# A third attention head of a graph layer turned by 32x32 squares and transfers, in half-head pieces

## The chip, the cores and the metric

The kernel runs on one core of a Trainium2 chip. TensorE (PE) multiplies matrices and transposes, VectorE (DVE) and ScalarE (ACT) work element by element and empty TensorE's accumulation banks (PSUM), GpSimd (POOL) does some additions, and SyncE (SP) issues the transfers (DMA). Times are device microseconds of one launch. The median of three runs before is 3433.64 us, and the runs lie between 3432.25 and 3434.13.

## The reference, cut to what matters

A batch of 32 graphs, each with 512 nodes and 256 channels, passes four layers of graph attention. After each layer the input is added and the sum is normalised over its channels:

```python
x = _layernorm(x + _L0_gnn_ref(x, adj, ...))   # "a": one head of 256 channels
x = _layernorm(x + _L1_gnn_ref(x, adj, ...))   # "b": transformer, 8 heads of 32
x = _layernorm(x + _L2_gnn_ref(x, adj, ...))   # "c": 4 heads of 64
x = _layernorm(x + _L3_gnn_ref(x, adj, ...))   # "d": bilinear scores, one head
```

The change is mainly in the third layer, c:

```python
q = (h @ W).reshape(B, N, H, D)                # H = 4, D = 64
e = e_src[:, :, None, :] + e_dst[:, None, :, :]
e = jnp.where(e >= 0, e, ALPHA * e)
e = jnp.where(mask, e, NEG_INF)
attn = jax.nn.softmax(e, axis=2)
h_prime = jnp.einsum('bijh,bjhd->bihd', attn, q)
```

For each head there is a 512 x 512 matrix of attention weights. The kernel holds it as four row blocks of 128 x 512. The last line sums over its columns, and TensorE sums over the partitions, so each of the four blocks has to be transposed before the weighted sum: this is what the kernel calls turning.

## The kernel before, in words

All values are float32. The program builds a list of operations (`op`), each with the engines that may run it, a planned cost, the buffers that it writes and reads, and a stage name: a letter for the layer and a digit (0 preparation, 1 scores, 2 finish, 3 softmax and turning, 4 weighted sum). `Plan.order` then lays the operations out engine by engine, with up to `WINDOW` = 4 graphs in work at once. Among ready operations it takes the one with the lowest key: graph number times `AGE` of the engine, less the length of the chain behind it, less `URGENT` of engine and stage; for TensorE a change of the matmul's form (full, tiled by rows, tiled by columns) costs `SWITCH_WEIGHT` times an entry of `SWITCH`. An operation that takes a buffer waits in the plan until one of the `BUFS` of its kind is free. The result is a fixed order for every engine; on the chip the engines follow their own lists and wait for each other by semaphores.

In layer c, `Gat.attend` (line 814) goes over two groups of two heads. For each head TensorE spreads a column of scores over a bank (line 835), VectorE adds the mask and takes each row's maximum (`masked`, line 684), and ScalarE applies the leaky slope (line 739) and the exponential (line 745) in place. Then `turned` (line 691) transposes in one of two ways:

- By TensorE: `turn` (line 580) makes four 128 x 128 transposes into a bank for each row block (line 586), and `copied` takes the bank to the turned buffer `pq` (ScalarE at line 529 or VectorE at line 531, as the planner decides).
- By squares and transfers: VectorE transposes every 32 x 32 square in place (line 702), once for each row block, and SyncE moves the squares to their places with 16 transfers of 64 KB for a head (line 714). Each transfer waits for all four row blocks, since a head's four blocks are one buffer `tq`, which is held from the masking until the last transfer has landed.

`BY_TRANSFERS` names the heads that go the second way: heads 2 and 3 of layer c, in all graphs but the last `PLAIN` = 2. A turned head is one `pq` buffer of 2048 words per partition. `weighted` (line 591) then multiplies for both heads of a group, four row blocks at once: 512 columns, in two column tiles of 64 side by side (line 603). The sum is copied to `oT`, transposed back for each half of the nodes (`turned_back`, line 610, instructions at line 619), and scaled into `y` (line 631). Layers a and d use `rows_weighted` (line 890, instructions at line 896), layer b `weighted` with 256 columns in four tiles of 32. Other lines that the numbers below name: 557 and 572 are projections, 806 the projection of layers a and c, 934 the scores of layer b and 948 and 955 their masking and exponential, 1072 the scores of layer d. SyncE also loads the inputs (line 358) and stores the output (line 1108), in the same order as the moves.

Of the kernel before, what the change touches and what calls it, by code (L numbers as in the profile page):

```python
# [24 lines left out]
SLOPE = 0.2  # L25


BUFS = dict(t=16, x=5, xT=3, v=5, qk=4, y=5, e=3, n=2, nT=2, hT=3, oT=2, tq=2, pq=5, small=8)
# [11 lines left out]
AGE = {"PE": 257, "ACT": 221, "DVE": -182, "POOL": 528, "SP": 151}  # L40
URGENT = {
    "PE": {"a0": -75, "a1": 707, "a2": 344, "b0": -756, "b1": 306, "b2": 700, "c0": -1085, "c1": -566, "c2": -26, "d0": -1544, "d1": -1472, "d2": -1512, "a3": 1865, "a4": 679, "b3": 269, "b4": -122, "c3": 3149, "c4": 468, "d3": -1054, "d4": 94},
    "ACT": {"a0": -877, "a1": 23, "a2": 412, "b0": 1122, "b1": 150, "b2": 22, "c0": 432, "c1": -809, "c2": -763, "d0": 680, "d1": -1928, "d2": -1182, "a3": 920, "a4": 701, "b3": 234, "b4": -604, "c3": 1629, "c4": 1505, "d3": -786, "d4": -337},
    "DVE": {"a0": 633, "a1": 670, "a2": 648, "b0": 1045, "b1": -236, "b2": -513, "c0": -2048, "c1": -657, "c2": 497, "d0": -1572, "d1": -869, "d2": -2025, "a3": 1551, "a4": 544, "b3": -1617, "b4": -331, "c3": 91, "c4": 1954, "d3": -1641, "d4": -1168},
    "POOL": {"a0": -1566, "a1": -815, "a2": 2482, "b0": 1576, "b1": -742, "b2": -986, "c0": -744, "c1": -1896, "c2": 3131, "d0": 1272, "d1": 1709, "d2": -1760, "a3": -1181, "a4": 746, "b3": -824, "b4": 1874, "c3": -105, "c4": 2168, "d3": 1794, "d4": 2316},
    "SP": {"a0": 578, "a1": -291, "a2": 1436, "b0": -478, "b1": -110, "b2": -662, "c0": -380, "c1": -1000, "c2": 35, "d0": 1115, "d1": -375, "d2": -249, "a3": 144, "a4": 71, "b3": -603, "b4": 627, "c3": -231, "c4": 1331, "d3": 989, "d4": -515},
# [6 lines left out]
SWITCH_WEIGHT = 869  # L53
# [5 lines left out]
DMA_US = 0.63  # L59
# [3 lines left out]
BY_TRANSFERS = {"a": (), "b": (), "c": (2, 3), "d": ()}  # L63
# [247 lines left out]
def gnn_stack(  # L311
# [188 lines left out]
    class Rows:  # L500


        def __init__(self, buf, cell=None):
            self.buf, self.cell = buf, cell
            self.use = buf if cell is None else (buf, cell)

        def __call__(self):
            return self.buf[:] if self.cell is None else self.buf[:, self.cell]

    def rows(n, name, together=False):  # L510

        if together:
            t = buf("tq", [P, n, N], name, n)
            return [Rows(t, i) for i in range(n)]
        return [Rows(buf("t", [P, N], f"{name}_{i}")) for i in range(n)]
# [64 lines left out]
    def turn(t, pT, pcell, to, name):  # L580

        ps = bank([P, NB, P], name)

        def issue(e):
            for j in range(NB):
                nc.tensor.transpose(ps[:, j], t()[:, block(j)], ident)  # L586

        op({PE: 0.44}, issue, [ps], [t.use], [pT])
        copied(N, to, lambda: ps[:], [(pT, pcell)], [ps])
# [20 lines left out]
    def turned_back(oT, n, y, name, f=None):  # L610


        ps = bank([P, FB, n, P], f"{name}_o")

        def issue(e):
            for i in range(FB):
                for c in range(n):
                    o = oT[:, c, block(i)] if f is None else oT[:, f * FB + i]
                    nc.tensor.transpose(ps[:, i, c], o, ident)  # L619

        op({PE: 0.225 * n}, issue, [ps], [oT], [y])
        return ps
# [57 lines left out]
    def masked(s, t, top, i):  # L680


        def issue(e):
            nc.vector.tensor_tensor_reduce(  # L684
                out=t(), in0=s[:], in1=neg[:, i], scale=1.0, scalar=LOWEST, op0=ALU.add,
                op1=ALU.max, accum_out=top[:, i : i + 1],
            )

        op({DVE: 0.61}, issue, [t.use, (top, i)], [s, (neg, i)])

    def turned(ts, pT, blocks, by_transfers, name):


        if not by_transfers:
            for i in blocks:
                turn(
                    ts[i], pT, i, lambda i=i: pT[:, i * NB : (i + 1) * NB], f"{name}_tr{i}"
                )
            return

        for i in blocks:
            op({DVE: FLIP_US}, lambda e, t=ts[i]: nc.vector.transpose(t(), t()), [ts[i].use], [])
        t = ts[0].buf

        def squares():
            return t[:].rearrange("p i (j n) -> p (i j) n", n=P)

        for a in range(P // SQ):
# [6 lines left out]

            op({SP: P // SQ * DMA_US}, move, [(pT, a)], [t], lag=2.0)

    def leaky_softmax(ts, top, v, src, total, at, blocks, name):
# [17 lines left out]
        for i in blocks:  # L736

            def leaky(e, i=i, t=ts[i]):
                nc.scalar.activation(  # L739
                    t(), t(), AF.Prelu, alpha=SLOPE,  # L740
# [3 lines left out]
            def exp(e, i=i, t=ts[i]):  # L744
                nc.scalar.activation(  # L745
                    t(), t(), AF.Exp, bias=bias[:, i : i + 1],
# [3 lines left out]
            op({ACT: 0.53 if src is None else 0.62}, leaky, [ts[i].use], [] if src is None else [v])  # L750
            op({ACT: 0.71}, exp, [ts[i].use, (total, at * NB + i)], [bias])
# [30 lines left out]
    class Gat(Layer):  # L782
# [31 lines left out]
        def attend(self):  # L814
            H, D, name, v = self.H, C // self.H, self.name, self.v
            G = min(H, P // D) if H > 1 else 1
            for g in range(0, H, G):
# [3 lines left out]
                for h in range(G):  # L821
# [5 lines left out]
                    ts = rows(NB, f"{name}_t{g}{h}", by_transfers)  # L827
                    pT = buf("pq", [P, NB * NB, P], f"{name}_pT{g}{h}", NB)
# [8 lines left out]
                    o = op({PE: 0.44}, issue, [dst], [v], [t.buf for t in ts])  # L837
# [6 lines left out]
                    turned(ts, pT, range(NB), by_transfers, f"{name}_{g}{h}")  # L844
                    pTs.append(pT)
                op({DVE: 0.1}, lambda e, a=inv, b=total: nc.vector.reciprocal(a[:], b[:]), [inv], [total])
                plan.stage = name[0] + "4"
                if H > 1:
                    pv = bank([P, N], f"{name}_pv{g}")
                    oT = buf("oT", [P, NB, P], f"{name}_oT{g}")  # L850
                    weighted(
                        pv, oT, pTs,
                        lambda h, j, pTs=pTs: pTs[h][:].rearrange(
                            "p (i j) n -> p i j n", j=NB
                        )[:, :, j],
                        v, g * D, D, 3.55,
                    )
                    copied(
                        N, lambda oT=oT: oT[:].rearrange("p i n -> p (i n)"), lambda pv=pv: pv[:],
                        [oT], [pv],  # L860
                    )
                for f in range(F):
                    y = self.part_y(f)
                    plan.stage = name[0] + "4"
                    if H > 1:
                        ps = turned_back(oT, 1, y, f"{name}_{g}{f}", f)
                        op({DVE: 0.4}, scaled(y, f, g * D, ps, inv, D), [y], [ps, inv])
                    else:
                        pv = bank([P, FB, C], f"{name}_pv{f}")
                        rows_weighted(pv, pTs[0], v, y, f)  # L870
# [19 lines left out]
    def rows_weighted(pv, pT, v, y, f):  # L890

        for i in range(FB):

            def issue(e, i=i):
                for j in range(NB):
                    nc.tensor.matmul(  # L896
                        pv[:, i], lhsT=pT[:, (f * FB + i) * NB + j], rhs=v[:, j, 0:C],
# [3 lines left out]
            reads = pT if BY_TRANSFERS[y.name[0]] else (pT, f * FB + i)  # L901
            op({PE: 1.73}, issue, [pv], [reads, v], [y])

    class Transformer(Layer):
# [14 lines left out]
        def attend(self):  # L919
            name, q_sb, k_sb = self.name, self.q, self.k  # L920
            for f in range(F):
# [4 lines left out]
                for c in range(NC):  # L926
                    ts = [rows(Q, f"{name}_t{f}{c}{i}") for i in range(FB)]
                    for i in range(FB):
                        ss = [bank([P, N], f"{name}_s{f}{c}{i}{q}") for q in range(Q)]

                        def scores(e, i=i, ss=ss, c=c, f=f):
# [8 lines left out]
                            {PE: 0.95}, scores, ss, [(q_sb, f), k_sb], [t.buf for t in ts[i]],  # L940
                            form="rows",
                        )
                        for q in range(Q):
# [3 lines left out]
                            def reduce(e, i=i, h=h, t=t, s=s, f=f, low=low):  # L947
                                nc.vector.tensor_tensor_reduce(  # L948
                                    out=t(), in0=s[:], in1=neg[:, f * FB + i],
# [4 lines left out]
                            def exp(e, i=i, h=h, t=t, low=low, total=total):  # L954
                                nc.scalar.activation(  # L955
                                    t(), t(), AF.Exp, bias=low[:, i, h : h + 1], scale=-1.0,
# [241 lines left out]
```

## Time and profile before

| | us |
|---|---|
| median of three runs | 3433.64 |
| time of the profiled execution | 3431.66 |
| its span, from first to last instruction | 3429.9 |
| TensorE busy | 3397.8 |
| VectorE busy | 2922.9 |
| ScalarE busy | 2785.3 |
| GpSimd busy | 854.4 |
| share of the 16 DMA engines' time taken by transfers that SyncE issued | 16.0% |

"Busy" is the time in which an engine had at least one instruction under way. For TensorE that is no measure of use: its matmuls overlap, and a matmul's mean time in a row is longer than the distance between two of them. "PEld" is its weight load, which runs beside the matmuls. A row of an instruction group gives line, engine, operation, what is written from what, shapes and count, then busy time and the mean of one instruction, then the idle time of the engine just before such instructions and what ended it. In a view by order of time a line has the start, the time from the first start to the last end, the engine, and the instructions merged into it. SyncE's lines give the time that the issue of a transfer took there; the transfer itself lands later.

### The profile page before, as it was taken

How to read it: one execution, taken by the hardware profiler on the slowest of the kernel's cores; microseconds unless marked ns; L12 is line 12 of the kernel's file. 1: busy time of each engine (PE TensorE's matmuls, PEld its weight loads, DVE VectorE, ACT ScalarE, POOL GpSimd, SP SyncE). 2: the span in 40 equal slices, each digit the busy share in tenths (PEclk: the TensorE clock that was granted, in tenths of full speed). 3: DMA queues.
4: the chain of work that ended last, by engine and by line, in shares of the span. 5: the costliest groups of instructions: out<-in, count | busy, mean ns of one | idle time of the engine just before them, and what ended most of it. 6: DMA issues, size and time to landing. Idle time of an engine off the chain costs nothing.

```text
span 3429.9 us, 65651 instructions
## 1 busy us (share of the span) xinstructions
PE 3397.8 (99%) x22744; PEld 2531.6 (74%) x22744; DVE 2922.9 (85%) x8645; ACT 2785.3 (81%) x6747; POOL 854.4 (25%) x840
## 2 busy tenths in 40 slices
PE   8999999999999999999999999999999999999998
PEld 6766777777777777777777777777777777777766
DVE  7889888888888888898888888888888889888886
ACT  6788788888788888888787888878888888878785
POOL 1222132222222222222223222222222222222322
PEclk9999999999999999999999999999999999999999
DMA  2012111121121220112211112102122011221100
GB/s 95 11 26 44 30 28 36 40 44 37 20 43 33 44 44 18 39 32 44 44 31 26 37 39 44 38 19 44 32 44 44 18 39 32 44 44 31 26 20 19
DMA packets 563787, 122.17 MB, mean 36 GB/s; under 512 B 510848, under 2 KB 562688, under 8 KB 563456
## 3 DMA queue, kind: packets, MB, share of 16 engines
q1 hardware_dynamic: 563456, 117.98, 16.0%
q8 instruction: 181, 2.97, 0.4%
q14 instruction: 150, 1.23, 0.1%
HBM read 38.21 MB, written 16.78 MB: 16 GB/s over the span
## 4 chain that ended last, share of the span: by engine, by line
PE 97%; ACT 1%; DVE 1%; DMA 1%; issue 0%; SPq 0%; POOL 0%; POOLq 0%; DVEq 0%; ACTq 0%
PE ps L586 21%; PE ps L603 14%; PE ps L896 13%; PE ps L557 13%; PE ps L572 10%; PE ps L934 8%; PE ps L806 7%; PE ps L1072 6%; PE ps L542 3%; PE ps L835 2%; PE ps L619 2%; ACT tq L745 0%; ACT t L739 0%; ACT pq L529 0%; DMA xT<-in_x_T 0%
## 5 line engine op out<-in xcount | busy, mean ns | idle before, releaser
L586 PEld LDWEIGHTS ps<-ident,t 128*128 128x128 f32 x6208 | 696.7, 141 | 221.7 <-ACT t L955 72.8
L955 ACT ACTIVATE t<-t,low 128x512 f32<-128x512 f32 x1024 | 737.5, 732 | 132.6 <-DVE low L948 132.6
L586 PE MATMUL ps<-ident,t 128*128 128x128 f32 x6208 | 824.2, 276 | 6.1 <-ACT t L745 5.5
L529 ACT COPY pq<-ps 128x512 f32<-128x512 f32 x1054 | 573.1, 588 | 240.6 <-PE ps L586 239.9
L676 POOL TENSOR_TENSOR y<-y,x 128x512 f32<-128x512 f32 x256 | 328.1, 1282 | 1563.3 <-DVE y L631 676.8
L948 DVE CUSTOM_DVE_ANT_0 t<-ps,neg 128x512 f32<-128x512 f32 x1024 | 646.2, 683 | 50.5 <-PE ps L934 50.2
L656 POOL TENSOR_TENSOR rstd<-rstd,mhalf 128x2 f32<-128x2 f32 x384 | 281.3, 733 | 843.3 <-DVE rstd L653 827.5
L603 PE MATMUL ps<-pq,v 128*32 128x256 f32 (+1 forms) x5120 | 490.2, 425 | 0.6 <-issue 0.4
L896 PE MATMUL ps<-v,pq 128*128 128x256 f32 x2048 | 473.4, 379 | 0.7 <-ACT pq L529 0.7
L896 PEld LDWEIGHTS ps<-v,pq 128*128 128x128 f32 x2048 | 377.1, 190 | 47.7 <-ACT pq L529 1.1
L603 PEld LDWEIGHTS ps<-pq,v 128*32 128x32 f32 (+1 forms) x5120 | 210.5, 115 | 254.9 <-issue 127.2
L531 DVE COPY pq<-ps 128x512 f32<-128x512 f32 x498 | 326.4, 678 | 56.2 <-PE ps L586 55.9
L745 ACT ACTIVATE t<-t,bias 128x512 f32<-128x512 f32 x528 | 373.5, 708 | 0.1
L684 DVE CUSTOM_DVE_ANT_0 t<-ps,neg 128x512 f32<-128x512 f32 x528 | 338.2, 681 | 15.5 <-PE ps L1072 11.2
L739 ACT ACTIVATE t<-t,v 128x512 f32<-128x512 f32 x400 | 271.8, 716 | 56.4 <-DVE top L684 54.1
L650 DVE BATCH_NORM_STATS2 st<-y 128x6 f32<-128x256 f32 x768 | 285.3, 413 | 9.6 <-POOL y L676 9.4
L934 PE MATMUL ps<-qk,qk 32*128 32x512 f32 x2048 | 283.4, 633 | 0.0
L557 PE MATMUL ps<-xT,w_qkv_sb 128*128 128x256 f32 x1024 | 236.2, 379 | 1.0 <-ACT t L739 1.0
L1072 PE MATMUL ps<-xT,qk 128*128 128x512 f32 x512 | 235.9, 593 | 0.0
L557 PEld LDWEIGHTS ps<-xT,w_qkv_sb 128*128 128x128 f32 x1024 | 192.0, 190 | 26.2 <-ACT t L739 1.4
L955 ACT ACTIVATION_READ_ACCUMULATOR t<-t,low 128x1 f32 x1024 | 209.4, 205 | 0.0
L739 ACT ACTIVATE tq<-tq,v 128x512 f32<-128x512 f32 x240 | 159.8, 717 | 42.5 <-DVE top L684 42.5
(93 smaller groups left out, 5195.2 us busy)
## 6 DMA issues: line engine op xcount, KB each, us to landing
pq<-tq SPq DMA_DIRECT2D x960, 64.0 KB, 2.1
xT<-in_x_T SPq DMA_DIRECT2D x64, 256.0 KB, 3.3
x<-in_x SPq DMA_DIRECT2D x32, 512.0 KB, 4.0
out<-y SPq DMA_DIRECT2D x64, 256.0 KB, 2.1
t<-in_adj SPq DMA_DIRECT2D x4, 256.0 KB, 6.0
w_qkv_sb<-in_L_gnn_w_qkv SPq DMA_DIRECT2D x1, 768.0 KB, 6.4
w_sb<-in_L_gnn_w SPq DMA_DIRECT2D x2, 256.0 KB, 5.6
t<-in_L_gnn_W SPq DMA_DIRECT2D x2, 256.0 KB, 2.7
```

The lines of the kernel that those rows point to most:

```text
L529: nc.scalar.copy(dst(), ps())
L557: nc.tensor.matmul(ps[:, c], lhsT=w[:, k, lo + c * P : lo + (c + 1) * P], rhs=xT[:, k, nlo : nlo + FN], start=(k == 0), stop=(k == NC - 1),)
L572: nc.tensor.matmul(ps[:, i], lhsT=xT[:, k, nlo + i * P : nlo + (i + 1) * P], rhs=w[:, k, lo : lo + C], start=(k == 0), stop=(k == NC - 1),)
L586: nc.tensor.transpose(ps[:, j], t()[:, block(j)], ident)
L603: nc.tensor.matmul(at, lhsT=v[:, j, lo + h * D : lo + (h + 1) * D], rhs=p, start=(j == 0), stop=(j == NB - 1), skip_group_check=True,)
L739: nc.scalar.activation(t(), t(), AF.Prelu, alpha=SLOPE, bias=0.0 if src is None else v[:, i, src : src + 1],)
L745: nc.scalar.activation(t(), t(), AF.Exp, bias=bias[:, i : i + 1], accum_out=total[:, i, at : at + 1],)
L896: nc.tensor.matmul(pv[:, i], lhsT=pT[:, (f * FB + i) * NB + j], rhs=v[:, j, 0:C], start=(j == 0), stop=(j == NB - 1),)
L934: nc.tensor.matmul(s[:], lhsT=q_sb[at, c, block(f * FB + i)], rhs=k_sb[at, c], start=True, stop=True,)
L948: nc.vector.tensor_tensor_reduce(out=t(), in0=s[:], in1=neg[:, f * FB + i], scale=-1.0 / math.sqrt(D1), scalar=HIGHEST, op0=ALU.add, op1=A ...
L955: nc.scalar.activation(t(), t(), AF.Exp, bias=low[:, i, h : h + 1], scale=-1.0, accum_out=total[:, i, h : h + 1],)
L1072: nc.tensor.matmul(s[:], lhsT=hh[:, k, block(i)], rhs=xT[:, k], start=(k == 0), stop=(k == NC - 1),)
```

## The change

Four things are changed together:

1. Heads 1, 2 and 3 of layer c are turned by squares and transfers, not 2 and 3 only.
2. The flip of the squares is written to a buffer of its own. A `tq` buffer now holds half a head (two row blocks) and lives from the flip until its transfers have landed; before that a head uses four ordinary `t` buffers like every other. A half is moved by 16 transfers of 32 KB.
3. Turned weights are held by halves too: ten `pq` buffers of half the size, not five. The weighted sum of layer c, its copy and its transposition back are done for each half of the nodes, 256 columns at a time. In layer b a `pq` buffer holds one head, not two, for the same number of words.
4. The planner's constants and the numbers of buffers are others: `AGE`, `URGENT`, `SWITCH_WEIGHT`, the planned cost of a transfer (0.55, not 0.63), 18 `t` buffers and not 16, three `tq` (of half the size) and not two, three `oT` and not two, two `hT` and not three. So the order of all work changes.

```diff
-BUFS = dict(t=16, x=5, xT=3, v=5, qk=4, y=5, e=3, n=2, nT=2, hT=3, oT=2, tq=2, pq=5, small=8)
+BUFS = dict(t=18, x=5, xT=3, v=5, qk=4, y=5, e=3, n=2, nT=2, hT=2, oT=3, tq=3, pq=10, small=8)
...
-AGE = {"PE": 257, "ACT": 221, "DVE": -182, "POOL": 528, "SP": 151}
+AGE = {"PE": 420, "ACT": 765, "DVE": -353, "POOL": 896, "SP": 250}
...
-SWITCH_WEIGHT = 869
+SWITCH_WEIGHT = 277
...
-DMA_US = 0.63
+DMA_US = 0.55
...
-BY_TRANSFERS = {"a": (), "b": (), "c": (2, 3), "d": ()}
+BY_TRANSFERS = {'a': (), 'b': (), 'c': (1, 2, 3), 'd': ()}
...
-        for i in blocks:
-            op({DVE: FLIP_US}, lambda e, t=ts[i]: nc.vector.transpose(t(), t()), [ts[i].use], [])
-        t = ts[0].buf
+        flipped = buf("tq", [P, FB, N], f"{name}_q{f}", FB)
+        for k, i in enumerate(blocks):
+            op(
+                {DVE: FLIP_US}, lambda e, k=k, t=ts[i]: nc.vector.transpose(flipped[:, k], t[:]),
+                [(flipped, k)], [ts[i]],
+            )
...
-            op({SP: P // SQ * DMA_US}, move, [(pT, a)], [t], lag=2.0)
+            op({SP: P // SQ * DMA_US}, move, [(pT, a)], [flipped], lag=2.0)
+
+    def weights_T(name):
+
+        return [buf("pq", [P, FB * NB, P], f"{name}_{f}", NB) for f in range(F)]
...
-                    pv = bank([P, N], f"{name}_pv{g}")
-                    oT = buf("oT", [P, NB, P], f"{name}_oT{g}")
...
                     if H > 1:
-                        ps = turned_back(oT, 1, y, f"{name}_{g}{f}", f)
+                        pv = bank([P, FN], f"{name}_pv{g}{f}")
+                        oT = buf("oT", [P, 1, FN], f"{name}_oT{g}{f}")
+                        weighted(
+                            pv, oT, [pT[f] for pT in pTs],
+                            lambda h, j, f=f, pTs=pTs: pTs[h][f][:].rearrange(
+                                "p (i j) n -> p i j n", j=NB
+                            )[:, :, j],
+                            v, g * D, D, 1.86,
+                        )
+                        copied(FN, lambda oT=oT: oT[:, 0], lambda pv=pv: pv[:], [oT], [pv])
+                        ps = turned_back(oT, 1, y, f"{name}_{g}{f}")
                         op({DVE: 0.4}, scaled(y, f, g * D, ps, inv, D), [y], [ps, inv])
...
-                    pTs = [
-                        buf("pq", [P, 2 * NB, FN], f"{name}_pT{f}{c}{k}", 2 * FB)
-                        for k in range(Q // 2)
-                    ]
+                    pTs = [buf("pq", [P, NB, FN], f"{name}_pT{f}{c}{q}", FB) for q in range(Q)]
```

## The prediction

> **What bounds the kernel now.** I read the page's engine shares first, then the chain that ended last, then a table of busy time over stretches of the steady state, then TensorE's and SyncE's instructions in order of time.
>
> ```profile
> span 3429.9 us, 65651 instructions
> PE 3397.8 (99%) x22744; PEld 2531.6 (74%) x22744; DVE 2922.9 (85%) x8645; ACT 2785.3 (81%) x6747; POOL 854.4 (25%) x840
> ...
> PE 97%; ACT 1%; DVE 1%; DMA 1%; issue 0%; SPq 0%; POOL 0%; POOLq 0%; DVEq 0%; ACTq 0%
> ```
>
> A busy TensorE alone proves nothing; that 97% of the chain is TensorE says that nearly every step waited for the instruction before it on TensorE. Where the missing 32 us lie is told by the table of stretches (length; then busy us of TensorE, weight load, VectorE, ScalarE, GpSimd; granted clock; DMA share):
>
> ```profile
> 711.00:816.40 105.40, 105.40 (x709) 78.49 (x709) 90.66 (x271) 87.10 (x212) 26.63 (x26) 1.00 0.17 35
> 816.40:921.80 105.40, 105.40 (x709) 78.52 (x709) 90.64 (x271) 87.09 (x212) 26.61 (x26) 1.00 0.17 36
> ```
>
> One graph takes 105.40 us, again and again, and TensorE is busy in all of it at full clock. VectorE has 14.7 us to spare per graph, ScalarE 18. So in the middle TensorE work taken away is time won, as long as nothing else comes late; the idle time is in the first and last graphs.
>
> **What a transpose is worth.** The change takes 16 transposes per graph (one head, 4 row blocks of 4) from TensorE in 30 of 32 graphs: 480, in 120 calls of four. Four numbers compete:
>
> ```profile
> L586 PE MATMUL ps<-ident,t 128*128 128x128 f32 x6208 | 824.2, 276 | 6.1 <-ACT t L745 5.5
> ...
> by line: PE ps L586 20.7%; PE ps L603 13.8%; PE ps L896 12.8%; PE ps L557 12.6%; PE ps L572 9.6%; PE ps L934 7.6%; PE ps L806 6.5%; PE ps L1072 6.3%; PE ps L542 3.2%; PE ps L835 2.0%; PE ps L619 1.6%; issue 0.2%; ACT tq L745 0.2%; ACT t L73
> ```
> ```profile
> 1061.30 1.93 PE L603 MATMUL ps<-pq,v 128*32 128x256 f32 x32
> 1063.16 1.97 PE L586 MATMUL ps<-ident,t 128*128 128x128 f32 x16
> ...
> 1069.78 3.65 PE L603 MATMUL ps<-pq,v 128*64 128x512 f32 x16
> 1073.36 0.66 PE L586 MATMUL ps<-ident,t 128*128 128x128 f32 x4
> ...
> 1096.87 0.60 PE L586 MATMUL ps<-ident,t 128*128 128x128 f32 x4
> 1097.31 1.89 PE L896 MATMUL ps<-v,pq 128*128 128x256 f32 x8
> ```
>
> The 276 ns is the duration of one from issue to end; they overlap. Busy time by count is 824.2 / 6208 = 133 ns, but the end of each group is counted again under its successor (0.60 us shown, next start 0.44 later). Start to start, four take 0.44 us. The chain's share, which counts no moment twice, is 20.7% of 3429.9 = 710 us, 114 ns each. The Trainium skill (TensorE: Matmul & The Clock Gate, section PE-mode transpose) puts a 128x128 transpose in a running kernel at about 275 ns, most of it access latency. By that number 480 would be worth 132 us and the kernel would end near 3301; by start to start they are worth 120 x 0.44 = 53, by the chain 480 x 0.114 = 55, by busy time 64. I take the chain's **55 us**, with 53 to 64 as ends: latency is paid once per dependency, not per pipelined instruction.
>
> **What TensorE gets back.** The third layer's weighted sum, 64 calls of 512 columns, becomes 128 of 256. A full call takes 1073.36 - 1069.78 = 3.58 us. The nearest row for a short one is the second layer's call of 256 columns (1063.16 - 1061.30 = 1.86 us), with the same array time: four 32-wide tiles side by side do in it what two 64-wide ones do in half the columns. So two halves cost 3.72 at most, 3.58 at least: 0 to 9 us over 64 pairs; I take **9**. Changing the form of the matmul (full, row-tiled, column-tiled) shows as some 0.1 us (the eight matmuls of L572 take 1.83 us to the next start behind a column-tiled call and 1.73 otherwise). The new order has 792 such changes, the old one 736: 56 x 0.1 = **6 us**. Transposes of the result stay equal in number. Sum: -55 + 9 + 6 = **-40 us**.
>
> **VectorE and ScalarE.** 120 more flips at 157.6 / 240 = 0.657 us are 79 us for VectorE. 120 fewer copies out of PSUM are shared; in the new order VectorE has 65 fewer of them (0.655 us, from 326.4 / 498) but gets other copies and relus from ScalarE. Counting all instructions that change engine, with the rows' busy time each, VectorE gains 121 us (to 3044, 90%), ScalarE loses 94 (79%). The flips now wait for their buffer's earlier transfers too; the waiting instructions on VectorE rise by 597, at 0.021 to 0.050 us 13 to 30 us. Per graph VectorE comes to some 95.5 of 104 us. I cost it at nothing on the path because 8 us stay over. If that cover fails, the maskings (L684) and score reductions (L948) behind a waiting flip come late, and the next transposes on TensorE with them. Writing the flip out of place keeps its 512 columns and so its price; GpSimd's work is unchanged.
>
> **The transfers.** This is the part the trace does not show directly: 32 transfers of 64 KB per graph become 96 of 32 KB, all issued by SyncE in order, between the loads and stores.
>
> ```profile
> 1017.63 10.68 SPq L714 DMA_DIRECT2D pq<-tq  x16
> ...
> 1054.93 2.79 SPq L714 DMA_DIRECT2D pq<-tq  x4
> 1057.76 1.14 SPq L358 DMA_DIRECT2D xT<-in_x_T  x2
> 1058.94 8.53 SPq L714 DMA_DIRECT2D pq<-tq  x12
> ```
> ```profile
> L714 SPq DMA_DIRECT2D pq<-tq x960: 585/627/1864, 200.7 to 3281.3; - x192
> ...
> L358 SPq DMA_DIRECT2D xT<-in_x_T x64: 368/475/628, 1.7 to 3168.8; - x64
> L358 SPq DMA_DIRECT2D x<-in_x x32: 368/619/1325, 17.8 to 3177.4; - x32
> ...
> L1108 SPq DMA_DIRECT2D out<-y x64: 372/390/397, 318.7 to 3427.0; - x64
> ```
>
> The issue time follows the number of separate runs: 512 runs cost 0.627 (64 KB) and 0.619 us (512 KB), 256 runs 0.390 and 0.475. A new transfer has 32 x 8 = 256 runs. Against this stands a rule of the Trainium skill (DMA: Bandwidth & Descriptors, section Bandwidth): batch transfers, since below 64 KB they are dominated by descriptors, 64 KB taking 0.95 us and 4 KB still 0.68; measured there on GpSimd's queue from HBM. By it halving the size saves little, and an issue stays near 0.63. I take 0.45 by the rows, with 0.39 to 0.71 as ends, the upper one from the run of 12 above (8.53 / 12). Landing takes 2.1 us, as on the page.
>
> What does it meet? In the new order, priced with these rows, head 1's first half is moved 14.9 us of TensorE work ahead of the weighted sum that reads it: 16 x 0.45 + 2.1 = 9.3 us are needed. The sixth and last half of a graph is read 65.3 us of TensorE work after the first move; on the trace's scale (105.4 for 103.6 of my priced sum) that is 66.5. By 0.45 the issues take 43 us; the flips of the last half stand 38 us behind the first move and set its start, leaving it some 17 us early. The nearest flip stands 5.5 us behind the last issue that reads its buffer, against 2.1 to land. So I put **0 us** on the path. The DMA engines are no limit: packets go from 563 456 by 245 760 to 809 216, their share from 16% to 23%.
>
> **The forecast.** The sum is against the profiled execution: span 3429.9, its time 3431.66, which lies 2 us under the runs' median of 3433.64. -40 gives a span near 3390 and a median near **3393 us** (-1.2%), 104.1 us per graph. This case's own range, 3378 to 3405, is -55 (the gain with no return) to about -28 (all costs and 0.4 us of small stalls per graph).
>
> **Rivals.**
>
> *TensorE is held up in places by VectorE.* A flip that waits stops VectorE, 90% loaded and with no reordering, and TensorE's next transposes wait. For it: the slack per graph falls from 14.7 to about 8.5 us. Against it: TensorE did not wait once in the steady state before. A price of 0.7 us per graph, half of what is won, over 30 graphs is 21 us: near 3414, still faster.
>
> *The third head's transfers come too late.* One mechanism: SyncE's issue of a 256-run transfer costs as much as a 512-run one did, or more. The last half is then late by 96 d + 1.7 (two stores, two loads) + 2.1 - 66.5, and TensorE, which takes its weighted sums in order, stops there in each of 30 graphs. It begins at d = 0.653 us; the gain is eaten at 1.34 us per graph, d = 0.667; slower by more than 0.2% from 0.67. At 0.70, 4.5 us x 30 = 135 gives about 3528. For it: 16 issues in a row averaged 0.668 before, above their median of 0.627, and twelve 0.71; the skill's rule. Against it: both 256-run rows.
>
> *The transposes were covered anyway* (no change: 3427 to 3440). Against it: the chain is 21% L586, with hardly an idle moment ahead of it. It could only come about by two effects that happen to cancel.
>
> **How the numbers follow.** TensorE sets the pace and the gain arrives: 0.60. VectorE takes part of it (3405 to 3427): 0.17. About as before, within 0.2% (some 7 us, the least that a measurement here tells from no change): 0.05. Transfers late, slower: 0.18. Faster is 0.60 + 0.17 = 0.77. The range goes from 3378 (2 in 100 below) to 3440, which leaves out the slower case: 0.20 in all.
>
> **What would show it.** Right: stretches of about 104.1 us with TensorE busy throughout; 480 fewer transposes at the same start to start; the halves of the weighted sum at 1.8 to 1.9 us each; the issue of the small moves between 0.39 and 0.48 us; VectorE near 90%. Wrong: TensorE idle ahead of the weighted sum, released by a transfer; issues above 0.65 us; VectorE idle ahead of the flips until a transfer lands; a weighted half well over 1.86 us. The order of everything else changes as well, since the planner's weights do; if the steady state has TensorE gaps that no transfer ends, the new order is at fault, which no row here can price.

## The result and the profile after

The changed kernel takes 3564.92 us (median of four runs, 3562.77 to 3568.95) against 3432.94 for the kernel before on the same chip: 1.0386 times the time, with a 95% interval of 1.0368 to 1.0404. It is slower by 132 us, where 40 us less were forecast. Line numbers from here on are those of the changed kernel. Its lines for those of before are 573 for 586 (transposes by TensorE), 590 for 603 (weighted sum), 701 for 714 (moves), 688 for the flip, 669 and 934 for the maskings, 736 and 941 for the exponentials, 920 for 934 and 1054 for 1072 (scores of layers b and d), 544 for 557 and 797 for 806 (projections), 516 and 518 for 529 and 531 (copies). L529 is now a transposition by TensorE (542 before).

The head of the page and its chain:

```profile
span 3563.8 us, 69935 instructions
PE 3411.2 (96%) x23288; PEld 2555.7 (72%) x23288; DVE 3100.9 (87%) x8848; ACT 2707.4 (76%) x6608; POOL 856.6 (24%) x840
...
PE 49%; DVE 17%; SPq 15%; ACT 10%; DMA 5%; issue 4%; POOL 0%; DVEq 0%; POOLq 0%; ACTq 0%
```

The chain was 97% TensorE before. Half of it is now something else: 15% is SyncE issuing transfers, 5% transfers landing, 17% VectorE. Two graphs of the steady state, in the table of stretches (length; busy us of TensorE, weight load, VectorE, ScalarE, GpSimd; clock; DMA share):

```profile
1483.32:1593.00 109.68, 105.27 (x726) 79.13 (x724) 97.04 (x277) 84.19 (x206) 26.66 (x26) 1.00 0.23 44
1593.00:1702.34 109.34, 105.62 (x726) 79.12 (x724) 97.07 (x277) 84.17 (x206) 26.68 (x26) 1.00 0.23 45
```

A graph takes 109.5 us, not 104.1, and TensorE stands still for some 4 us of it; in these two graphs the granted clock is full (1.00), and the DMA engines are far from full. TensorE's waits (us in all, times, longest):

```profile
PE ps L590 <- DMA pq<-tq: 62.4, 40, 5.8
PE ps L797 <- DMA xT<-in_x_T: 25.0, 24, 1.9
PE ps L573 <- ACT t L736: 21.8, 28, 0.8
```

The first is the weighted sum waiting for squares. The second is the projection waiting for an input whose load stands behind the moves in SyncE's queue. The third has another source, as the experiments show. The first two add up to 87 us; the view of waits does not hold the whole loss (see e9). In order of time, SyncE over one graph, then TensorE at the end of that stretch:

```profile
1497.08 43.77 SPq L701 DMA_DIRECT2D pq<-tq  x64
1540.96 1.05 SPq L1090 DMA_DIRECT2D out<-y  x2
1542.12 1.00 SPq L358 DMA_DIRECT2D xT<-in_x_T  x2
1543.22 22.82 SPq L701 DMA_DIRECT2D pq<-tq  x32
```
```profile
1511.28 1.95 PE L590 MATMUL ps<-pq,v 128*64 128x256 f32 x16
1513.16 1.14 PE L920 MATMUL ps<-qk,qk 32*128 32x512 f32 x8
...
1567.58 1.91 PE L590 MATMUL ps<-pq,v 128*64 128x256 f32 x14 [2.54 <-DMA pq<-tq]
```

SyncE issues without a pause from 1497.08 to 1566.04. The 96 moves take 43.77 + 22.82 = 66.59 us, 0.694 each; the last one lands 1.5 us later and TensorE, which had waited 2.54 us, goes on. The duration of a single issue (least, median, longest, in ns) is

```profile
L701 SPq DMA_DIRECT2D pq<-tq x2880: 585/609/1957, 192.8 to 3423.4; - x192
```

The median is 0.609 us for 256 runs, where 512 runs took 0.627 and 0.45 was forecast. A weighted half takes 1513.16 - 1511.28 = 1.88 us, as forecast. The group row of the transposes has 480 fewer, at the same mean:

```profile
L573 PE MATMUL ps<-ident,t 128*128 128x128 f32 x5728 | 754.9, 276 | 23.2 <-ACT t L736 21.8 <-ACT t L941 1.0 <-ACT pq L516 0.4
```

Behind some of the waits a second, smaller loss shows. The granted clock of the whole span was 0.993 (0.999 before), and in short stretches it was 0.50, as here (TensorE in order of time, then the table of stretches):

```profile
2114.66 2.90 PE L590 MATMUL ps<-pq,v 128*64 128x256 f32 x14 [2.06 <-DMA pq<-tq]
...
2115.50:2118.80 3.30, 3.30 (x15) 2.10 (x12) 0.09 (x1) 1.08 (x3) 0.43 (x1) 0.50 0.33 113
```

After the wait at 1567.58 the same 14 matmuls took 1.91 us, here 2.90. Over the span this is worth at most (1 - 0.993) x 3563.8 = 25 us, against 3 before.

### The profile page after: what moved, and what is told of

Same layout as the page of the kernel before. It is cut to its first block, busy times and chain, and to the rows that moved or that the text cites. A ratio compares the mean times of both kernels' runs of the same rounds, so it can differ in the third digit from the quotient of the medians.

```text
span 3563.8 us, 69935 instructions
## 1 busy us (share of the span) xinstructions
PE 3411.2 (96%) x23288; PEld 2555.7 (72%) x23288; DVE 3100.9 (87%) x8848; ACT 2707.4 (76%) x6608; POOL 856.6 (24%) x840
## 4 chain that ended last, share of the span: by engine, by line
PE 49%; DVE 17%; SPq 15%; ACT 10%; DMA 5%; issue 4%; POOL 0%; DVEq 0%; POOLq 0%; ACTq 0%
SPq L701 15%; PE ps L573 9%; PE ps L883 9%; PE ps L559 8%; PE ps L544 7%; ACT t L941 6%; PE ps L590 5%; DVE t L669 4%; PE ps L797 4%; PE ps L920 3%; DVE st L635 3%; DMA pq<-tq 3%; ACT pq L516 3%; DMA xT<-in_x_T 3%; DVE rstd L638 1%
## 5 line engine op out<-in xcount | busy, mean ns | idle before, releaser
L573 PEld LDWEIGHTS ps<-ident,t 128*128 128x128 f32 x5728 | 644.8, 141 | 198.6 <-ACT t L941 79.3
L573 PE MATMUL ps<-ident,t 128*128 128x128 f32 x5728 | 754.9, 276 | 23.2 <-ACT t L736 21.8
L661 POOL TENSOR_TENSOR y<-y,x 128x512 f32<-128x512 f32 x256 | 330.9, 1293 | 1641.2 <-DVE top L718 781.6
L934 DVE CUSTOM_DVE_ANT_0 t<-ps,neg 128x512 f32<-128x512 f32 x1024 | 651.0, 683 | 32.7 <-PE ps L920 31.8
L590 PE MATMUL ps<-pq,v 128*32 128x256 f32 (+1 forms) x6144 | 533.7, 387 | 65.1 <-DMA pq<-tq 62.4
L736 ACT ACTIVATE t<-t,bias 128x512 f32<-128x512 f32 x768 | 543.8, 709 | 0.3
L730 ACT ACTIVATE t<-t,v 128x512 f32<-128x512 f32 x640 | 428.8, 715 | 115.7 <-DVE top L669 115.3
L669 DVE CUSTOM_DVE_ANT_0 t<-ps,neg 128x512 f32<-128x512 f32 x768 | 494.4, 682 | 11.4 <-PE ps L1054 8.2
L590 PEld LDWEIGHTS ps<-pq,v 128*32 128x32 f32 (+1 forms) x6144 | 277.8, 120 | 305.7 <-issue 93.3
L518 DVE COPY pq<-ps 128x512 f32<-128x512 f32 x433 | 285.8, 681 | 148.5 <-PE ps L573 144.0
L516 ACT COPY oT<-ps 128x256 f32<-128x256 f32 x145 | 53.5, 369 | 249.5 <-PE ps L590 249.5
L688 DVE STREAM_TRANSPOSE tq<-t 128x512 f32<-128x512 f32 x360 | 230.2, 682 | 5.3 <-DMA pq<-tq 5.0
```

Source lines behind the costliest of these rows:

```text
L516: nc.scalar.copy(dst(), ps())
L573: nc.tensor.transpose(ps[:, j], t[:, block(j)], ident)
L590: nc.tensor.matmul(at, lhsT=v[:, j, lo + h * D : lo + (h + 1) * D], rhs=p, start=(j == 0), stop=(j == NB - 1), skip_group_check=True,)
L669: nc.vector.tensor_tensor_reduce(out=t[:], in0=s[:], in1=neg[:, i], scale=1.0, scalar=LOWEST, op0=ALU.add, op1=ALU.max, accum_out=top[:, i ...
L730: nc.scalar.activation(t[:], t[:], AF.Prelu, alpha=SLOPE, bias=0.0 if src is None else v[:, i, src : src + 1],)
L736: nc.scalar.activation(t[:], t[:], AF.Exp, bias=bias[:, i : i + 1], accum_out=total[:, i, at : at + 1],)
```

## The experiments

The theory after the result was that the third head's transfers come too late (the forecast's slow rival). The other theories were that the new order of all work, or VectorE's load, is at fault. Except in e2 and e3, every kernel below keeps the order of the kernel it starts from on TensorE, VectorE and ScalarE; only e10 and e12 move operations, which they name.

### e1: the same order, a quarter of the issues

```diff
-                for b in range(P // SQ):
-                    there = slice(b * SQ, (b + 1) * SQ)
-                    nc.sync.dma_start(out=pT[there, :, here], in_=squares()[here, :, there])
+                nc.sync.dma_start(
+                    out=pT[here], in_=squares()[here]
+                )
```

> The changed kernel, with the four transfers of each step put together into one: SyncE issues 24 transfers of 128 KB for a graph and not 96 of 32 KB; bytes, buffers, waits and the order on TensorE, VectorE and ScalarE stay. The squares are left in their own partitions, so the turned weights of heads 1 to 3 are wrong and only the time counts. If SyncE's time per issue is the cause (96 x some 0.65 us = 63 us in series, so the last halves come too late), the issues of a graph take some 16 us, TensorE is busy throughout again and the time falls to 3385 to 3405. If VectorE's load or the new order of the work is the cause and late transfers only follow from it, it stays above 3500.

Measured: 3430.07 us, ratio 0.9984 (0.9978 to 0.9991). This lies between the two ranges expected. TensorE no longer waits for a transfer of squares. So the late transfers cost 135 us, but the time stops 37 us above the forecast. (The transfers of e1 are larger as well as fewer; e9 parts the two.) One graph, and TensorE's waits:

```profile
1528.34:1633.54 105.20, 104.17 (x726) 78.39 (x724) 96.53 (x277) 83.78 (x206) 26.73 (x26) 1.00 0.19 46
```
```profile
PE ps L573 <- ACT t L736: 23.5, 29, 1.8
...
PE ps L544 <- DVE nT L518: 6.9, 27, 0.3
```

Some 1.03 us per graph are missing, in one place, once per graph. There, TensorE first, then VectorE, then GpSimd:

```profile
1538.75 0.66 PE L573 MATMUL ps<-ident,t 128*128 128x128 f32 x4 [0.78 <-ACT t L736]
1539.66 0.70 PE L544 MATMUL ps<-nT,w_sb 128*128 128x256 f32 x2 [0.25 <-DVE nT L518]
```
```profile
1533.42 0.16 DVE L718 TENSOR_TENSOR top<-top,v 128x4 f32<-128x4 f32 x1
...
1535.97 1.21 DVE L718 TENSOR_TENSOR top<-top,v 128x4 f32<-128x4 f32 x1
```
```profile
1535.89 1.27 POOL L987 TENSOR_TENSOR n<-n,g_sb 128x512 f32<-128x512 f32 x1 [2.83 <-PE ps L529]
```

L718 adds four values per partition. It takes 0.16 us, but 1.21 when GpSimd began a multiplication of 512 values 0.08 us earlier, and both end together, at 1537.2. The softmax (L736) waits for L718's result, and TensorE's transposes for the softmax. This looks like a collision: VectorE waits for GpSimd's instruction to end. The Trainium skill (SBUF — State Buffer, section Who interferes with whom) states such a rule: a VectorE instruction with two inputs in SBUF contends with a GpSimd instruction that reads SBUF, and the one that started first holds the shared ports for its whole length. The two rows agree with it; e6, e10 and e11 test it.

### e5: long runs, the same 96 issues

The squares are laid together, so that each of 32 partitions has one run of 1 KB, where there were eight runs of 128 bytes; the weighted sum reads them in that layout.

```diff
-        flipped = buf("tq", [P, FB, N], f"{name}_q{f}", FB)
+        flipped = buf("tq", [P, R, FB * NB * SQ], f"{name}_q{f}", FB)
...
-                    nc.sync.dma_start(out=pT[there, :, here], in_=squares()[here, :, there])
+                    nc.sync.dma_start(out=by_square(pT)[there, a], in_=flipped[here, b])
```

> The changed kernel with squares laid next to each other in the flipped and the turned buffer, so that each of the 96 transfers of 32 KB consists of 32 runs of 1 KB and not of 256 of 128 B; the order of the work stays, the weighted sum reads the squares with a longer access pattern. If an issue has a price for the transfer, whatever its runs: it stays at 0.58 to 0.63 us and the time within 1% of 3565. If the runs make the price (as my prediction had it, 0.39 to 0.48 for 256 runs): issues of 0.35 to 0.45 us and 3385 to 3430.

Measured: 3491.89 us, ratio 1.0166 (1.0151 to 1.0182). SyncE's lines of its moves (L705 in this kernel) in order of time, and the duration of a single issue:

```profile
1513.91 22.28 SPq L705 DMA_DIRECT2D pq<-tq  x32
...
1576.85 42.39 SPq L705 DMA_DIRECT2D pq<-tq  x64
```
```profile
L705 SPq DMA_DIRECT2D pq<-tq x2880: 507/588/2192, 193.7 to 3350.4; - x192
```

The median issue is 0.588 us with 32 runs, 0.609 with 256 (after), 0.627 with 512 (before). An eighth of the runs takes off 3.4%. So in these moves the price goes by the transfer, hardly by its runs, as the first of the two expectations had it; but the time fell by 2%, further than it allowed. Small as the saving is, it counts: 64.67 us per graph instead of 66.59 are 1.9 less, over 30 graphs 58 of the 73 us gained. The rest was not traced; the granted clock was 0.996, where after had 0.993, which by itself can be worth up to some 11 us.

### e9: the same transfers from two queues

```diff
-                    nc.sync.dma_start(out=pT[there, :, here], in_=squares()[here, :, there])
+                    (nc.gpsimd if b == 3 else nc.sync).dma_start(out=pT[there, :, here], in_=squares()[here, :, there])
```

> The changed kernel, right in all its results, with every fourth move issued by GpSimd's queue and not by SyncE's: 72 and 24 issues for a graph. SyncE's chain is then 72 x 0.686 = 49 us and not 66. If SyncE's issues in series are the cause, the weighted sums are in time: 3425 to 3450, as long as GpSimd, busy 25%, issues a transfer in about 1 us (24 us for a graph). If an issue on GpSimd costs much more, or if it waits there behind the additions, near 3565 or slower.

Measured: 3429.81 us, ratio 0.9988 (0.9981 to 0.9994). GpSimd's issues are as long as SyncE's:

```profile
L701 SPq DMA_DIRECT2D pq<-tq x2160: 585/609/1931, 193.1 to 3281.8; - x197
L701 POOL DMA_DIRECT2D pq<-tq x720: 582/584/767, 193.4 to 3282.4; - x180
```

With the same 2880 transfers of the same size, 135 us are gone, and no wait for squares is left. It was one queue's time to issue, not the DMA engines: the rule that the Trainium skill gives for spreading transfers (DMA: Bandwidth & Descriptors, section Rules for kernel authors: no bandwidth, only issue time) fits it. The rows of layer c's weighted sum, after and then e9, tell where the 135 us stood:

```profile
L590 PE MATMUL ps<-pq,v 128*64 128x256 f32 x2048 | 289.5, 397 | 64.8 <-DMA pq<-tq 62.4 <-issue 2.4
...
L590 PE MATMUL ps<-pq,v 128*64 128x256 f32 x2048 | 251.6, 388 | 0.1
```

65 us are idle time before the sums and 38 us stand in their busy time, in part at the lower clock; 24 more are the late inputs (L797, 25.0 us in after, 1.4 in e9). Waits alone would have shown two thirds of the loss. The whole of the lower clock can be no more than 18 of the 135 us (granted 0.993 and 0.998).

### e6 and e7: GpSimd's additions made small

In L661, L987, L988 and L991 GpSimd works on 4 columns, not on 512; e6 has the transfers of e1, e7 the 96 of the kernel after.

```diff
-            lambda e: nc.gpsimd.tensor_add(y[:], y[:], x[:, part(f)]),
+            lambda e: nc.gpsimd.tensor_add(y[:, 0, 0:4], y[:, 0, 0:4], x[:, f * FB, 0:4]),
```

> The kernel of e1 (24 large transfers), with GpSimd's additions and multiplications of 128 x 512 elements (layers' residual sums, gain and shift in layer b) cut to 4 columns, so they leave out nearly all of that work. In e1 TensorE works 104.1 us of a graph's 105.2 and waits 1.03 in one place, behind 21 us of uninterrupted VectorE work in which three small sums (lines 638 and 718) take 0.91, 0.46 and 1.21 us and not 0.16 because GpSimd has a large addition under way. If these collisions are what is left between e1 (3430) and the forecast (3393): the wait is gone, 30 x 1.03 = 31 us, 3388 to 3402, and line 718 is back at 0.17 us (0.34 in e1). If the flips' load on VectorE or the order of the work is what is left: 3422 to 3432.

> The changed kernel with all its 96 transfers, and GpSimd's operations cut to 4 columns as in e6. If the late transfers and the collisions cost each for itself: 3565 less some 25 to 40 us, 3525 to 3540. If the transfers come late mainly since VectorE is late with the flips: below 3460.

Measured: e6 3378.67 us, ratio 0.9838 (0.9824 to 0.9853); e7 3507.38, ratio 1.0216 (1.0200 to 1.0232). In e6 a graph takes 103.66 us with TensorE busy in all of it, and VectorE's small sums are short again:

```profile
1503.21:1606.87 103.66, 103.66 (x725) 78.50 (x724) 93.28 (x277) 83.81 (x206) 11.60 (x26) 1.00 0.19 47
```
```profile
L638 DVE TENSOR_TENSOR rstd<-mv,eps 128x2 f32<-128x2 f32 x384 | 61.6, 160 | 13.3
...
L718 DVE TENSOR_TENSOR top<-top,v 128x4 f32<-128x4 f32 x160 | 25.1, 157 | 0.0
```

e6, which leaves work out, fell below its range (3388 to 3402); e7 fell further than expected (3525 to 3540). The two costs nearly add up, in either order:

| us | 96 issues on SyncE | 24 issues | difference |
|---|---|---|---|
| GpSimd's additions whole | 3564.9 (after) | 3430.1 (e1) | 135 |
| GpSimd's additions cut | 3507.4 (e7) | 3378.7 (e6) | 129 |
| difference | 58 | 51 | |

But cut additions also finish earlier, so e6 alone does not tell a collision from a late addition.

### e8: is it VectorE's load?

e1 with every flip cut to a quarter of its columns.

```diff
-                lambda e, k=k, t=ts[i]: nc.vector.transpose(flipped[:, k], t[:]),
+                lambda e, k=k, t=ts[i]: nc.vector.transpose(flipped[:, k, 0:P], t[:, 0:P]),
```

> The kernel of e1 with each flip cut to a quarter of its columns (the rest of its buffer is set to zero once at the start): VectorE has some 12 x 0.48 = 5.8 us less to do for a graph, order and waits as in e1. If VectorE's load by the flips is what keeps e1 from the forecast: 3390 to 3405. If it is the stretch of VectorE work that holds the collisions, in which there is no flip: 3422 to 3432.

Measured: 3428.56 us, ratio 0.9986 (0.9980 to 0.9993). VectorE has 128 us less to do (2959.3, not 3087.2) and the time is that of e1. So the flips' load on VectorE is not what costs here. The stretch of VectorE work that holds the collisions has no flip in it, so e8 says nothing of the other work there; e11 leaves all of that in place.

### e10, e11 and e12: the collision taken away, all work done

All three start from e9. In e10 GpSimd does the two small sums itself, at the same place of the order:

```diff
-            nc.vector.tensor_tensor(rstd[:], mv[:, :, 1], eps, ALU.add)
+            nc.gpsimd.tensor_tensor(rstd[:], mv[:, :, 1], eps, ALU.add)
...
-                lambda e: nc.vector.tensor_tensor(top[:], top[:], v[:, :, src], ALU.add), [top], [v],
+                lambda e: nc.gpsimd.tensor_tensor(top[:], top[:], v[:, :, src], ALU.add), [top], [v],
```

In e11 they stay on VectorE, and GpSimd's large operations are cut in four (L987, L988 and L991 likewise):

```diff
-            lambda e: nc.gpsimd.tensor_add(y[:], y[:], x[:, part(f)]),
+            lambda e: [nc.gpsimd.tensor_add(y[:, i, k], y[:, i, k], x[:, f * FB + i, k]) for i in range(FB) for k in (slice(0, P), slice(P, C))],
```

> The kernel with one square in four on GpSimd's queue, and with the two small additions of VectorE (the variance's epsilon, L638, and the query's logit onto the row maxima, L718) done by GpSimd at the same place of the order; nothing is left out. If it is these two that wait for GpSimd's large additions and so make the 1.0 us hole per graph and more, the time falls by 31 us (30 graphs of 1.03 us) to 51 us (what cutting GpSimd's additions gave): 3379 to 3399, under the kernel before. If GpSimd, busier by 544 small operations of about 0.2 us and with these now behind its own additions in one queue, passes the delay on instead, the time stays within 10 us of 3430.

> The kernel with one square in four on GpSimd's queue, and each of GpSimd's 128x512 additions and multiplications of the norms (L661, L987, L988, L991) made as four of 128x128; nothing is left out. If VectorE's operation waits for the end of the one GpSimd instruction that is running, the longest wait falls from 1.27 us to an estimated 0.5 us and most of the gain of 51 us comes: about 3395. If it waits until GpSimd has none ready, the four in a row delay it as one does, and with more GpSimd time in all it is 3430 or slower.

Measured: e10 3389.87 us, ratio 0.9875 (0.9859 to 0.9892); e11 3387.45, ratio 0.9867 (0.9853 to 0.9882). Both beat the kernel before. One graph of e10, and a wait that it has more of than e9 (3.5 us there):

```profile
1514.36:1618.01 103.65, 103.65 (x725) 78.47 (x724) 92.23 (x261) 83.71 (x206) 43.80 (x67) 1.00 0.23 47
```
```profile
DVE st L635 <- POOL y L661: 31.1, 87, 1.6
```

In e11 the four pieces take longer than one did, 4 x 0.463 = 1.85 us against 1.29, but each holds VectorE for less:

```profile
L661 POOL TENSOR_TENSOR y<-y,x 128x128 f32<-128x128 f32 x1024 | 442.9, 463 | 1022.5 <-DVE top L718 397.9 <-DVE y L1076 269.4 <-DVE y L871 208.5
...
L718 DVE TENSOR_TENSOR top<-top,v 128x4 f32<-128x4 f32 x160 | 25.8, 161 | 0.0
```

This separates the two readings of e6. In both kernels the additions come later than in e9 (by VectorE's wait for L661 in e10, by their length in e11), and both are faster; what they have in common is that VectorE's small sum no longer stands behind a long GpSimd instruction. With all work done the collisions cost 40 us (e9 against e10) to 42 (against e11); of the 51 to 58 that e6 and e7 show, the rest may come from the work left out. Counting all 544 sums of L638 and L718 by the view in order of time, those over 0.25 us, and how much they lie above 0.16 us in all:

| kernel | stretched sums | us above 0.16 |
|---|---|---|
| before | 64 (L718's: 2) | 20 |
| after | 164 (28) | 84 |
| e9 | 166 (30) | 80 |
| e6 | 0 | 0 |
| e11 | 97 (3) | 34 |

Collisions are not new. New is that the order puts the logit sum of a softmax beside L987 in nearly every graph. Other VectorE operations are stretched too: the normalisation L649 (`x<-y,mv,rstd`) has a mean of 479 ns in after, 404 in e6 and 417 in e11. In e10 it stays at 475 and the time falls by 40 us all the same, so what was on TensorE's path are the sums.

> e10 and e11 together: one square in four on GpSimd's queue, GpSimd's additions in quarters, and the two small sums of L638 and L718 on GpSimd. In both TensorE is already busy 1399.9 us of 1400 in the middle of the span, so the second measure should find nothing left: 3384 to 3391. Below 3380 would say that waits are left which the view of TensorE's busy time doesn't show; above 3395, that GpSimd's queue has become a limit.

Measured for the two together: 3408.69 us, ratio 0.9929 (0.9913 to 0.9946), not what was expected; together they are worse than either. TensorE waits again in the old place, and VectorE's norm waits twice as long for GpSimd's root as in e10 (20.4 us there), the first line TensorE's, the second VectorE's:

```profile
PE ps L573 <- ACT t L736: 17.0, 29, 2.3
...
DVE n L649 <- POOL rstd L641: 41.0, 32, 1.4
```

GpSimd, with additions a half longer and the sums behind them in its one queue, passes the delay on. That this is the whole cause was not tested further.

### e13: is it the change that gains?

The kernel before with GpSimd's operations cut in four as in e11, in its own order.

```diff
-            lambda e: nc.gpsimd.tensor_add(y[:], y[:], x[:, part(f)]),
+            lambda e: [nc.gpsimd.tensor_add(y[:, i, k], y[:, i, k], x[:, f * FB + i, k]) for i in range(FB) for k in (slice(0, P), slice(P, C))],
```

> The kernel before, two heads by transfers, with GpSimd's additions and multiplications (L661, L987, L988, L991 of the kernel after) made as four of 128x128 each; nothing left out, its own order kept. The gain of e11 over the kernel before may be the change's or only that of the smaller additions. In the kernel before TensorE has no idle time in the middle of the span (1400.00 of 1400 us), so I expect nothing: 3428 to 3438. If the kernel before too loses time to VectorE's waits, it falls below 3425.

Measured: 3438.98 us, ratio 1.0016 (1.0009 to 1.0024). The smaller pieces bring the kernel before nothing, rather 5 us of loss. The 46 us by which e11 beats the kernel before are the change's: third head, halves and order together.

### e2 and e3: one part alone, with a new plan

e2 is the kernel after with two heads by transfers, e3 the kernel before with three.

```diff
-BY_TRANSFERS = {'a': (), 'b': (), 'c': (1, 2, 3), 'd': ()}
+BY_TRANSFERS = {'a': (), 'b': (), 'c': (2, 3), 'd': ()}
```

> The changed kernel with heads 2 and 3 alone turned by transfers, planned anew; halves, buffers and the planner's weights stay. If the time per issue is the cause: 64 x 0.65 = 42 us for a graph, nothing late, and 3430 plus some 15 us for the split weighted sum and the changes of form: 3435 to 3460. If halves, buffers or planner's weights are the cause, with two heads as with three: 3530 or more.

> The kernel before with head 1 added to the heads turned by transfers, and nothing else: whole heads, in place, 48 transfers of 64 KB for a graph. If the number of issues is the cause: 48 x 0.66 = 32 us for a graph, 16 fewer transposes, no split: 3375 to 3405. If a third head is too much for VectorE (the flips) or for two tq buffers held from the masking on: 3433 or slower.

Measured: e2 3720.45 us, ratio 1.0837 (1.0819 to 1.0855); e3 3894.34, ratio 1.1336 (1.1319 to 1.1353). Neither came out as expected, and neither isolates anything: other operations give the planner another order, and its weights were found for another set (presumably the reason; not tested). TensorE waits in many places at once, in e2 for squares too, though it moves 64 a graph; then e3, whose lines have the numbers of before:

```profile
PE ps L590 <- DMA pq<-tq: 78.2, 40, 3.5
PE ps L529 <- DVE x L649: 65.9, 12, 6.1
```
```profile
PE ps L586 <- ACT t L745: 101.4, 46, 10.7
PE ps L542 <- DVE x L664: 84.2, 16, 10.8
```

The granted clock was lower too, 0.980 in e2 and 0.954 in e3, which can be worth up to 74 and 179 us of the 286 and 459 lost. In e3 three heads also share two `tq` buffers that are held from the masking on, a cause that its expectation named and that no run parts from the order. What they show is that a part of the change, planned anew, can be 8 to 13% slower, so that only kernels with the same order tell what a part is worth.

## Why the prediction was wrong

**The step that failed** is "I take 0.45 by the rows, with 0.39 to 0.71 as ends". The rows of 256 runs were loads and stores between device memory and 128 partitions; the moves go from 32 partitions to 32, within SBUF. Their own row, 0.627 us at 512 runs, was nearer in kind, and the runs of 12 and 16 in a row (0.71 and 0.668) were the only ones that showed a queue under pressure. What the forecast drew from the Trainium skill (DMA: Bandwidth & Descriptors, section Bandwidth) and set aside, that halving a small transfer saves little, came true: 0.627 became 0.609. The page's own figures are for the transfer, though, not for its issue, so they could not settle it. With 0.694 from start to start, the forecast's own formula, 96 d + 1.7 + 2.1 - 66.5, gives 3.9 us per graph; with the measured 2.4 us for stores and loads and 1.9 to land it is 66.6 + 2.4 + 1.9 - 66.5 = 4.4, over 30 graphs 131. e1 and e9 against after measure 135, e6 against e7 129. So "0 us on the path" should have been +131, and the rival "the third head's transfers come too late", given 0.18 and 3528 us at 0.70, had the mechanism and the size. The order itself was planned with 0.55 us a transfer; whether one planned with 0.69 would have left room was not tried.

**The second step that failed** is "VectorE and ScalarE ... I cost it at nothing on the path because 8 us stay over". The rival "TensorE is held up in places by VectorE" named the flips and the load as its source; e8 refutes the flips' load. In its place the runs show the two-input sums of VectorE waiting for GpSimd's additions, 40 to 42 us with all work done (e9 against e10 and e11); the rival's 21 us was too low. The remark that "GpSimd's work is unchanged" was true and hid it: what counts is which instruction it falls beside, and the order decides that. The sign was there before the change, in the row of L718's counterpart (least, median and longest in ns), where TensorE was never idle in the middle of the span:

```profile
L727 DVE TENSOR_TENSOR top<-top,v x160: 148/156/1061, 21.7 to 3373.5; 128x4 f32<-128x4 f32 x160
```

A longest of 1.06 us against a median of 0.156, but then in 2 of 160 sums, later in 28.

**What held.** The TensorE sum of -40 us, 104.1 us per graph: without the two costs a graph takes 103.65 us (e10, e11), so 105.40 - 103.65 = 1.75 us less, and e11 ends at 3387 where 3393 was forecast. Summing the time from each matmul's start to the next by line, over ten graphs of before and of e10, gives for the 16 transposes 1.95 us per graph, 122 ns each (114 forecast by the chain's share, not the 276 ns of one's duration), so 58 us over 30 graphs. (The 275 ns of the page that the forecast cites are for bf16; here a transpose of f32 took 276.) The halves took 1.88 us each; the line of all weighted sums grew by 0.18 us per graph, so some 5 us (9 forecast). All other lines together, which would hold the 6 us for changes of form, balance to 0.02 us per graph. So the return of 15 us was put too high. Over the whole run e11 gains 46 us and not 52; by subtraction the rest lies outside the steady graphs. VectorE came to 90% once nothing else held it (e1), the DMA engines were no limit (23%). The sum of packets was short: 839 936 and not 809 216, which is 16 more for each of the 1920 added transfers.

**The sum of it:** 3387 to 3390 with neither cost (e11, e10); + 40 to 42 (collisions, to e9) + 135 (issues, from e9 to after) = 3565. Such a chain of differences closes by itself; that the two costs are separate is what e6 and e7 show.

What stays open: why a move within SBUF has a higher price of issue than a load of as many runs (partitions, direction and memory differ at once, and no run parted them), why its distance from start to start goes from 0.66 to 0.71 in full queues when its median is 0.61, and what lowers the clock in short stretches: those looked at follow a wait of TensorE of some 2 us (2.06 above), but none of the runs was made for it.

## What to carry to other kernels

When work is moved to a queue that issues transfers one after another, count the queue's time per round, at the start-to-start distance that the same kind of transfer shows in a full queue, against the time at which the last one is needed; if it is late, try a second queue or fewer transfers first: here they brought 135 us, and transfers with an eighth of the runs 73. Before an order is judged by the load of its engines, look for short instructions whose longest duration is many times the median: here a four-column sum of 0.16 us that fell beside a GpSimd multiplication took 1.21 and held TensorE up by 1 us per graph. Undo one part of a planned kernel only with the plan held fixed.

## What the runs showed of the hardware beyond the expected

- A transfer of 32 KB from 32 partitions to 32 costs its queue 0.588 us with 32 runs and 0.609 with 256, one of 64 KB with 512 runs 0.627, and GpSimd's queue 0.584; loads and stores over 128 partitions with 256 runs cost 0.390 to 0.475 (medians, before).
- VectorE's sum of two small SBUF operands took up to 1.22 us beside GpSimd's 1.27 us operation, at most 0.49 (L718) or 0.6 (L638, but once 2.36) beside pieces of 0.46 us. VectorE's row maxima over PSUM (L669) kept a median of 682 to 685 ns in after, e1, e10 and e11 alike.
- The granted clock was 0.50 in short stretches, ten of them in after, and 1.00 otherwise; 14 matmuls of the weighted sum took 2.90 us there and 1.91 elsewhere.
